# Two-layer state-space vision block: column stores collected over a whole image, images held in pairs of chunks, first tap by channel tile, one table load for 1 / std in the last image

## The chip, the cores and the metric

The kernel runs on one core of a Trainium2 chip. The metric is the device time of one execution in microseconds; the time of a kernel is the median of its runs. The profile comes from one further execution, whose own time is given beside its span.

## What is computed

The input x has 8 images of 64 x 64 positions and 192 channels. Two layers follow each other; each adds to x the output of one block applied to the group-normalized x (32 groups). Cut to what matters, with D = 384 inner channels and L = 4096 positions of an image:

```python
xz = einsum('bhwc,ec->bhwe', gn(x), in_proj_w); xx, z = split(xz)
xc = silu(depthwise_conv3x3(xx) + conv_b)
xs = directions(xc)           # rows, rows reversed; layer 1 also columns, columns reversed
dts, Bs, Cs = split(x_proj_weight @ xs)
delta = softplus(dt_w @ dts + dt_b)
h = exp(delta * A) * h + (delta * u) * B      # step by step along the L positions, 16 states
y = sum(h * C) + xs * Ds                      # summed over the directions
y = layernorm(y) * ln_w + ln_b
x = x + out_proj_w @ (y * gate(z))            # gate: gelu in layer 0, silu in layer 1
```

Layer 0 scans in two directions (along rows, both ways), layer 1 in four (rows and columns, both ways). So layer 1 needs xc in two orders: by rows (`xcd`) and by columns (`xcd_col`).

## The kernel before

The work of each layer is a front and then scans, one layer after the other. The four parts run on the same core; a layer's scans begin when its front has ended.

**Tiling.** An image is cut into 8 chunks of T = 512 positions (8 rows of 64). The 384 inner channels are three channel tiles (dt) of 128 partitions. The 192 input channels lie in `x1` (the first 128 on 128 partitions, 16 KB each) and `x2` (the other 64, with even chunks on the lower and odd chunks on the upper 64 partitions). Both are held for a whole image, twice (`bufs=2`). `load(b)` (L232) reads an image with four DMAs for x1 and two for x2, all on SP's queue.

**The front** (`front`, L206) is under a manual schedule: each engine runs its instructions in the order in which `order()` (L414) emits them. The loop there takes one pair of chunks, 2p and 2p+1, per pass (32 passes for 8 images). A pass holds, in this order:

- `conv(b, 2p)` (L357): the later taps of the depthwise convolution as block-diagonal matmuls into `pc`, then the sum of the first taps (`tp`) added through the mask matrix; Silu on ACT into `xo`; the store of `xo` to `xcd` on SP's queue. In layer 1, ACT then copies each channel tile of the chunk, turned to columns, into `xw` (L377). An `xw` tile covers four chunks (`HC = 4`); with the fourth, ACT issues its store to `xcd_col` (L384), in runs of 32 floats.
- for each channel tile: `project` (L315) of the next pair, which is four matmul groups into two of the four `pi` buffers and two copies into `pad` (on DVE, and on ACT for the third tile in layer 0); `turn` (L386) of the chunk before, which transposes a tile of `xo` on PE into a `pi` buffer and copies it to `xv` on ACT.
- in layer 0 `x_proj` (L400) of the chunk before.
- `first` (L342) of the next pair's first chunk: the first tap on ACT, for all three channel tiles; `second` (L349): the other early taps on DVE, three per channel tile in layer 1 and four in layer 0. They read `pad` and build `tp`.
- `conv(b, 2p+1)`, `turn` of chunk 2p, in layer 0 `x_proj` of chunk 2p, and `first` and `second` of the next pair's second chunk; the third channel tile's `second` of that chunk is left for the next pass.

Between these stand the steps for the next image's group statistics: `stats` (L251, DVE, 12 per image), `means`, `group_means` and `variances` (L267 to L295, with small matmuls that spread the group values and a Sqrt on ACT, which needs a table load), and `normalize` (L297, ACT, in place on x1 and x2). `load(b + 2)` is issued in pass p=2.

**The scans** (`scans`, L503) go through steps of one chunk in one direction. A dictionary of slots sets the place of each function within a step; `L0_SLOTS`, `L0_LAST`, `L1_SLOTS` and `L1_LAST` hold the slot numbers. Per slot, a decay Exp on ACT (L712), a scan on DVE (L736), a product on POOL (L737) and matmuls on PE run together. Ready output chunks go through the `f_` functions. In the last image (`last`), whose chunks are finished one per step, `f_rstd` (L884) computes 1 / std as Exp(-0.5 Ln(v)), and `f_act` (L893) applies the gate to z. In layer 0, `f_act` is in slot 18 and `f_rstd` in slot 19. In layer 1 they are in slots 22 and 17. `dt_softplus` (L629) ends with a preload of the table set that holds ln and exp.

Of the kernel before, what the change touches and what calls it, by code (L numbers as in the profile page):

```python
# [8 lines left out]
F32 = mybir.dt.float32  # L9
# [6 lines left out]
P = 128  # L16
B = 8
H = 64
W = 64
L = H * W  # L20
# [4 lines left out]
DT = 3  # L25
NS = 16
T = 512
# [6 lines left out]
NP = NS // 2  # L34
NG = NS // 2
S = (G + 1) * NG
HC = 4
GN_EPS = 1e-5
LN_EPS = 1e-5

# [165 lines left out]
def front(tc, name, x_src, xcd, xcd_col, xtd, xdd, w_in, t, clear, consts):  # L206
# [9 lines left out]
    with tc.tile_pool(name=f"{name}_a1", bufs=1) as a1, tc.tile_pool(  # L216
# [12 lines left out]
                nc.vector.tensor_scalar_mul(taps[:, dt, s - NV, :], mask, cw[:, dt, s : s + 1])  # L229
        ims = {}  # L230

        def load(b):  # L232

            im = ims[b] = {
                "x1": a2.tile([P, L], F32, name="x1"),
                "x2": a2.tile([P, NH, T], F32, name="x2"),
                "bst": a2.tile([P, NCH + NH, 6], F32, name="bst"),
            }
            for q in range(4):
                sl = slice(q * (L // 4), (q + 1) * (L // 4))  # L240
                nc.sync.dma_start(out=im["x1"][:, sl], in_=x_src[b][:P, sl])
            for r in range(2):
                nc.sync.dma_start(
                    out=im["x2"][r * G : (r + 1) * G],
                    in_=x_src[b][P:].rearrange("p (c r t) -> r p c t", r=2, t=T)[r],
                )

        def part_of(im, n):
            return im["x1"][:, n * T : (n + 1) * T] if n < NCH else im["x2"][:, n - NCH]

        def stats(b, *ns):  # L251
            for n in ns:
                nc.vector.bn_stats(ims[b]["bst"][:, n], part_of(ims[b], n))
# [61 lines left out]
        def project(b, p, dt):  # L315

            im = ims[b]
            pi = [psa.tile([P, T], F32, name="pi", bufs=4) for r in range(2)]
            cols = slice(dt * P, (dt + 1) * P)
            for r in range(2):  # L320
                nc.tensor.matmul(  # L321
                    pi[r], w_x1[:, cols], part_of(im, 2 * p + r), start=True, stop=False
                )
            for r in range(2):
                rows = slice(r * G, (r + 1) * G)
                nc.tensor.matmul(
                    pi[r],
                    w_x2[rows, cols],
                    im["x2"][rows, p],
                    start=False,  # L330
                    stop=True,
                    tile_position=(r * G, 0),
                )
            for r in range(2):
                c = 2 * p + r
                copy = nc.scalar.copy if dt == 2 and xdd is not None else nc.vector.tensor_copy
                copy(
                    pad[:, dt, 1 + c * RB : 1 + (c + 1) * RB, 1 : W + 1],
                    pi[r].rearrange("p (h w) -> p h w", w=W),
                )  # L340

        def first(b, c):  # L342

            tp = ims[b]["tp", c] = a2.tile([P, DT, T], F32, name="tp")
            for dt in range(DT):
                tv = tp[:, dt].rearrange("p (h w) -> p h w", w=W)
                nc.scalar.activation(tv, window(dt, c, 0), AF.Identity, scale=cw[:, dt, 0:1])  # L347

        def second(b, c, *dts):  # L349
            for dt in dts:  # L350
                tv = ims[b]["tp", c][:, dt].rearrange("p (h w) -> p h w", w=W)
                for s in range(1, NV):
                    nc.vector.scalar_tensor_tensor(  # L353
                        tv, window(dt, c, s), cw[:, dt, s : s + 1], tv, ALU.mult, ALU.add
                    )

        def conv(b, c):  # L357
            pc = psa.tile([P, DT, T], F32, name="pc")
            for s in range(NV, 9):
                for dt in range(DT):  # L360
                    block_diag(
                        nc, pc, taps[:, dt, s - NV, :], window(dt, c, s), dt, s == NV, False
                    )
            for dt in range(DT):
                block_diag(nc, pc, mask, ims[b]["tp", c][:, dt], dt, False, True)
            xo = ims[b]["xo", c] = a2.tile([P, DT, T], F32, name="xo")
            for dt in range(DT):
                nc.scalar.activation(xo[:, dt], pc[:, dt], AF.Silu, bias=cb[:, dt : dt + 1])  # L368
            nc.sync.dma_start(out=xcd[b].rearrange("(t p) l -> p t l", p=P)[:, :, c * T : (c + 1) * T], in_=xo)
            if xcd_col is None:  # L370
                return
            part, at = divmod(c, HC)
            if at == 0:
                ims[b]["xw"] = [a2.tile([P, W, HC * RB], F32, name="xw", bufs=5) for dt in range(DT)]
            for dt in range(DT):
                xw = ims[b]["xw"][dt]
                nc.scalar.copy(  # L377
                    xw[:, :, at * RB : (at + 1) * RB],
                    xo[:, dt].rearrange("p (h w) -> p w h", w=W),
                )  # L380
                if at == HC - 1:
                    xwv = xcd_col[b].rearrange("(t p) (w h) -> p t w h", p=P, h=H)
                    rows = slice(part * HC * RB, (part + 1) * HC * RB)
                    nc.scalar.dma_start(out=xwv[:, dt, :, rows], in_=xw)  # L384

        def turn(b, c, dt):  # L386
            im = ims[b]
# [25 lines left out]

        def order():  # L414

            stats(0, *range(NCH + NH))
            means(0)
            group_means(0)
            deviations(0)
            variances(0)  # L420
            normalize(0, 0)
            for dt in range(DT):
                project(0, 0, dt)
            for c in range(2):
                first(0, c)
                second(0, c, *range(DT))
            normalize(0, 1, 2, 3)
            if B > 1:
                load(1)
            early_stats = ((4, 5), (8, 9)), ((), (4, 5, 6, 7))  # L430
            late_stats = ((6, 7), (10, 11)), ((0, 1, 2, 3), (8, 9, 10, 11))
            prev = None
            for g in range(B * NH):
                b, p = divmod(g, NH)
                more = b + 1 < B
                n, q = divmod(g + 1, NH)
                go = g + 1 < B * NH
                conv(b, 2 * p)
                for dt in range(DT):
                    if go:  # L440
                        project(n, q, dt)
                    if dt == 0 and prev:
                        second(b, 2 * p + 1, 2)
                    if prev:
                        turn(*prev, dt)
                    if p == 2 and more and dt == 1:
                        group_means(b + 1)
                if p == 2 and more:
                    deviations(b + 1)
                if prev and xdd is not None:  # L450
                    x_proj(*prev)
                if go:
                    first(n, 2 * q)
                    second(n, 2 * q, *range(DT))
                if p < 2 and more:
                    stats(b + 1, *early_stats[b == 0][p])
                conv(b, 2 * p + 1)
                for dt in range(DT):
                    turn(b, 2 * p, dt)
                if xdd is not None:  # L460
                    x_proj(b, 2 * p)
                if p == 2 and more:
                    variances(b + 1)
                    normalize(b + 1, 0)
                if go:
                    first(n, 2 * q + 1)
                    second(n, 2 * q + 1, 0, 1)
                if p < 2 and more:
                    stats(b + 1, *late_stats[b == 0][p])
                if p == 1 and more:  # L470
                    means(b + 1)
                if p == 3 and more:
                    normalize(b + 1, 1, 2)
                if p == 0 and b:
                    normalize(b, 3)
                if p == 2 and b + 2 < B:
                    load(b + 2)
                if p == 3 and b + 2 < B:
                    stats(b + 2, *range(4))
                prev = b, 2 * p + 1  # L480
            for dt in range(DT):
                turn(*prev, dt)
            if xdd is not None:
                x_proj(*prev)

        load(0)
        if clear:
            zero = a1.tile([P, T * S // G // 8], F32, name="zero")
            nc.gpsimd.memset(zero, 0.0)
# [13 lines left out]
def scans(tc, name, x_src, x_dst, xcd, xcd_col, xtd, xdd, t, dirs, rank, row_b, gate, slots, last, consts, dram):  # L503
# [33 lines left out]
    with tc.tile_pool(name=f"{name}_s1", bufs=1) as s1, tc.tile_pool(  # L537
# [352 lines left out]
                fin["y"], fin["y"], fin["pv"].unsqueeze(1).to_broadcast([P, DT, T])  # L890
            )

        def f_act():  # L893
            nc.scalar.activation(fin["g"], fin["g"], gate)

        def f_affine(dt):
            nc.scalar.activation(  # L897
# [92 lines left out]
        for c in range(NCH):  # L990
# [20 lines left out]
            for w, (src, key) in enumerate((("y", "pm"), ("sq", "pv"))):  # L1011
                thrice(e, own["f_mean"][w], f_mean, src, key)
            for f in f_center, f_square, f_rstd, f_scale, f_act:
                at(e, own[f.__name__], f, *((c == NCH - 1,) if f is f_square else ()))
            for dt in range(DT):
                at(e, own["f_affine"][dt], f_affine, dt)
                at(e, own["f_times"][dt], f_times, dt)
# [144 lines left out]
```

## Time and profile before

| | us |
|---|---|
| runs, median of 3 | 26029.92 (26021.06 to 26032.92) |
| profiled execution, own time | 26028.44 |
| its span, first to last instruction | 26026.6 |
| front of layer 0 | some 20 to 985 |
| front of layer 1 | some 9192 to 10317 |
| an image in the front of layer 0 (between equal places in successive images) | 119.6 |
| an image in the front of layer 1 (mean of seven) | 138.1 |

Over the whole span PE is busy for 24190.1 us (93%), DVE 24270.1 (93%), POOL 22104.7 (85%) and ACT 17787.7 (68%). These shares are those of the scans, which fill most of the span. The front has to be read in stretches of its own. A line of a timeline gives the start, the time from the first start to the last end of the merged instructions, the engine, the line of the kernel, and in brackets the idle time before it with what ended it. PEq, ACTq and SPq are the engines' instruction queues: time spent on issuing a DMA is there. A line of a chain gives the start, the length and what ran; the chain is the work that ended last, followed back.

### The profile page before, as it was taken

To read this page: it belongs to the slowest core of one execution; us is meant where nothing else is said; L and a number is where in the kernel's file an instruction comes from. 1 tells how busy PE (TensorE), PEld (TensorE's weight loads), DVE (VectorE), ACT (ScalarE), POOL (GpSimd) and SP (SyncE) were. 2 spreads that over 40 slices of the span, in tenths; PEclk is the share of its full clock that TensorE was granted. 3 is DMA by queue.
4 is the path that set the end of the run, shared out by engine and by line. 5 is a ranking of instruction groups with operands and counts; after the bars stand their busy time and mean duration, and the time that the engine had idled before them with its cause. 6 is when DMAs were issued, how large, how long until landed. Compare 5 with 4: busy or idle time off the path is not lost.

```text
span 26026.6 us, 785972 instructions
## 1 busy us (share of the span) xinstructions
PE 24190.1 (93%) x340032; PEld 13575.8 (52%) x340032; DVE 24270.1 (93%) x22142; ACT 17787.7 (68%) x28084; POOL 22104.7 (85%) x9615
## 2 busy tenths in 40 slices
PE   8999999999999877999999999999999999999999
PEld 4455555555555533555555555555555555555554
DVE  7899999999999855999999999999999999999998
ACT  4567777777777655666767767767767767767766
POOL 0399999999999701999999999999999999999997
PEclk9999999999999988999999999999999999999999
DMA  4566666666666556576576576576576576576574
GB/s 153 145 154 158 153 154 154 155 158 155 156 155 154 136 149 159 163 161 166 164 164 166 164 163 166 163 163 166 163 164 167 163 163 167 164 163 167 164 163 140
DMA packets 4225339, 4140.59 MB, mean 159 GB/s; under 512 B 2532524, under 2 KB 2732868, under 8 KB 4221892
## 3 DMA queue, kind: packets, MB, share of 16 engines
q1 hardware_dynamic: 3819760, 4032.72, 60.1%
q10 hardware_dynamic: 402132, 57.59, 1.3%
q8 instruction: 2692, 44.11, 0.7%
q14 instruction: 755, 6.18, 0.1%
HBM read 3443.63 MB, written 645.99 MB: 157 GB/s over the span
## 4 chain that ended last, share of the span: by engine, by line
PE 40%; DVE 38%; ACT 10%; issue 9%; ACTq 1%; DMA 1%; POOL 0%; SPq 0%; DVEq 0%; POOLq 0%
DVE h L736 33%; PE hb L695 17%; PE py L152 11%; ACT da L712 3%; PE pt L608 2%; PE pz L835 2%; PE pd L560 2%; PE po L912 2%; DVE tp L353 2%; DVE dut L658 1%; ACT delta L145 1%; ACT L145 1%; PE pc L152 1%; ACT L632 1%; ACTq L384 1%
## 5 line engine op out<-in xcount | busy, mean ns | idle before, releaser
L737 POOL TENSOR_TENSOR hc<-h,cr 128x1024 f32<-128x1024 f32 x9216 | 21639.8, 2370 | 3773.7 <-DMA xt_k<-xtd 2178.2
L736 DVE TENSOR_TENSOR_SCAN h<-da,st,hb 128x512 f32<-128x512 f32 x16128 | 19187.5, 1258 | 629.8 <-PE hb L695 560.6
L712 ACT ACTIVATE da<-delta,a_neg 128x512 f32<-128x512 f32 x18432 | 12142.9, 713 | 3225.2 <-DVE h L736 3218.7
L695 PEld LDWEIGHTS hb<-dg,dut 64*128 64x128 f32 x147456 | 9260.3, 186 | 7083.1 <-issue 5877.6
L695 PE MATMUL hb<-dg,dut 64*128 64x128 f32 x147456 | 10909.6, 287 | 908.9 <-DVE h L736 639.5
L152 PE MATMUL py<-hc,mask 32*32 32x512 f32 x147456 | 6882.8, 603 | 0.2
L152 PEld LDWEIGHTS py<-hc,mask 32*32 32x32 f32 x147456 | 1571.9, 103 | 2348.3 <-issue 1770.6
L736 DVE TENSOR_TENSOR_SCAN h<-da,hb 128x512 f32<-128x512 f32 x2304 | 2611.8, 1199 | 135.1 <-PE hb L695 122.4
L742 ACT COPY st<-h 128x6 f32<-128x6 f32 x2688 | 532.9, 198 | 1844.2 <-DVE h L736 1843.7
L353 DVE SCALAR_TENSOR_TENSOR tp<-pad,cw,tp 128x512 f32<-128x512 f32 x1344 | 991.0, 750 | 592.3 <-ACT tp L347 537.8
L608 PE MATMUL pt<-xdbl,w_dt 96*128 96x512 f32 (+1 forms) x2304 | 1302.9, 647 | 49.5 <-DVE yc L878 34.9
L650 PE MATMUL pq<-ident,delta 128*128 128x128 f32 x4608 | 760.4, 288 | 387.7 <-DVE dut L658 333.7
L622 ACT ACTIVATE delta<-pt,dtb 128x512 f32<-128x512 f32 x1152 | 783.9, 681 | 485.4 <-PE pt L608 485.3
L835 PE MATMUL pz<-xn_sq,w_in 96*128 96x512 f32 x1536 | 826.1, 637 | 38.0 <-ACT xn_sq L823 14.8
L658 DVE TENSOR_TENSOR dut<-pq,xt_k 128x512 f32<-128x512 f32 x1152 | 765.8, 665 | 88.2 <-PE pq L650 88.2
L560 PE MATMUL pd<-x_k,w_x 128*128 128x512 f32 x1536 | 798.3, 629 | 30.9 <-DVE yc L878 15.1
L912 PE MATMUL po<-yc,w_out 128*96 128x512 f32 x1536 | 787.4, 624 | 16.8 <-POOL yc L906 15.0
L650 PEld LDWEIGHTS pq<-ident,delta 128*128 128x128 f32 x4608 | 485.2, 141 | 586.9 <-DVE dut L658 472.7
L321 PE MATMUL pi<-x,w_x 128*128 128x512 f32 x768 | 427.0, 664 | 313.7 <-ACT x L301 124.1
L906 POOL TENSOR_TENSOR yc<-yc,g 128x512 f32<-128x512 f32 x384 | 491.0, 1281 | 126.4 <-ACT yc L897 123.6
L152 PE MATMUL pc<-pad,taps 32*32 32x512 f32 x13824 | 575.9, 592 | 12.2 <-ACT xo L368 12.2
L145 ACT ACTIVATE delta<-delta 128x1536 f32<-128x1536 f32 x384 | 570.5, 1486 | 4.3
(105 smaller groups left out, 9921.3 us busy)
## 6 DMA issues: line engine op xcount, KB each, us to landing
cr<-cscr SPq DMA_DIRECT2D x2048, 512.0 KB
dg<-dgd SPq DMA_DIRECT2D x1536, 512.0 KB
cr<-xdd SPq DMA_DIRECT2D x1024, 512.0 KB
xt_k<-xtd SPq DMA_DIRECT2D x768, 384.0 KB
xcd<-xo SPq DMA_DIRECT2D x128, 768.0 KB
xtd<-xv SPq DMA_DIRECT2D x128, 768.0 KB
y<-yrow SPq DMA_DIRECT2D x128, 768.0 KB
yc<-yrow SPq DMA_DIRECT2D x128, 768.0 KB
```

Source lines behind the costliest of these rows:

```text
L145: nc.scalar.activation(out, in_, AF.Softplus)
L152: nc.tensor.matmul(out[j * Q : (j + 1) * Q, dt], w[i * Q : (i + 1) * Q], x[i * Q : (i + 1) * Q], start=first, stop=last, tile_position=(i ...
L353: nc.vector.scalar_tensor_tensor(tv, window(dt, c, s), cw[:, dt, s : s + 1], tv, ALU.mult, ALU.add)
L560: nc.tensor.matmul(live[i]["pd"][:R], w_x[:, dt, k, :], live[i]["x"][:, dt], start=(dt == 0), stop=(dt == DT - 1),)
L608: nc.tensor.matmul(pt, w_dt[:, k, dt * P : (dt + 1) * P], live[i]["xdbl"][:rank], start=True, stop=True,)
L650: nc.tensor.transpose(pq[:, g], live[i]["delta"][:, dt, g * P : (g + 1) * P], ident)
L695: nc.tensor.matmul(hv[:, r, q], live[i]["dut"][r * G : (r + 1) * G, dt, q], dg[r * G : (r + 1) * G, q, :, 2 * mm : 2 * mm + 2], start=True ...
L712: nc.scalar.activation(da[:, n].rearrange("p (r g j) -> p r g j", r=2, j=G), live[i]["delta"][:, dt].rearrange("p (g r j) -> p r g j", r=2 ...
L736: nc.vector.tensor_tensor_scan(o, a, v, init, ALU.mult, ALU.add)
L737: nc.gpsimd.tensor_mul(hc[:, dt], h[:, dt], live[i]["cr", m])
L835: nc.tensor.matmul(fin["pz"], w_in[:, u, dt * P : (dt + 1) * P], fin["xn"][:, u], start=(u == 0), stop=(u == CT - 1),)
L912: nc.tensor.matmul(fin["po"][:CP], w_out[:, dt, u * CP : (u + 1) * CP], fin["y"][:, dt], start=(dt == 0), stop=(dt == DT - 1),)
```

## The change

1. `load` takes pairs of chunks. `x1` and `x2` become tiles of one pair (4 KB and 2 KB a partition) with six buffers each. A pair is read with one DMA for x1 and two for x2. Pairs 0 and 1 of the next image but one are read at the end of pass p=3, pairs 2 and 3 of the next image in pass p=0. The order of the statistics follows, and none is left in p=3.
2. The copies to columns leave `conv` and become `columns(b, p)`, which takes both chunks of the pair after `conv(b, 2p+1)`, the turns and `x_proj`. An `xw` tile covers the whole image, with one buffer per channel tile, and its store is issued in p=3.
3. `first` takes channel tiles and is called behind each tile's `project` and `turn`. `second` of chunk 2p+1 is left for the next pass for the last two channel tiles, behind the projections.
4. In the last image, `f_act` ends with a preload of the table set with ln and exp.

```diff
-        def load(b):
+        def load(b, *ps):
+            im = ims.setdefault(b, {})
+            for p in ps:
+                if p == 0:
+                    im["bst"] = a2.tile([P, NCH + NH, 6], F32, name="bst")
+                im["x1", p] = a2.tile([P, 2 * T], F32, name="x1", bufs=6)
+                im["x2", p] = a2.tile([P, T], F32, name="x2", bufs=6)
+                sl = slice(2 * p * T, 2 * (p + 1) * T)
+                nc.sync.dma_start(out=im["x1", p], in_=x_src[b][:P, sl])
+                for r in range(2):
+                    nc.sync.dma_start(
+                        out=im["x2", p][r * G : (r + 1) * G],
+                        in_=x_src[b][P:, (2 * p + r) * T : (2 * p + r + 1) * T],
+                    )
...
-        def first(b, c):
+        def first(b, c, *dts):
+            if 0 in dts:
+                ims[b]["tp", c] = a2.tile([P, DT, T], F32, name="tp")
+            for dt in dts:
+                tv = ims[b]["tp", c][:, dt].rearrange("p (h w) -> p h w", w=W)
                 nc.scalar.activation(tv, window(dt, c, 0), AF.Identity, scale=cw[:, dt, 0:1])
...
+        def columns(b, p):
             if xcd_col is None:
                 return
-            part, at = divmod(c, HC)
-            if at == 0:
-                ims[b]["xw"] = [a2.tile([P, W, HC * RB], F32, name="xw", bufs=5) for dt in range(DT)]
+            if p == 0:
+                ims[b]["xw"] = [a2.tile([P, W, H], F32, name="xw", bufs=DT) for dt in range(DT)]
             for dt in range(DT):
                 xw = ims[b]["xw"][dt]
-                if at == HC - 1:
-                    nc.scalar.dma_start(out=xwv[:, dt, :, rows], in_=xw)
+                for c in 2 * p, 2 * p + 1:
+                    nc.scalar.copy(
+                        xw[:, :, c * RB : (c + 1) * RB],
+                        ims[b]["xo", c][:, dt].rearrange("p (h w) -> p w h", w=W),
+                    )
+                if p == NH - 1:
+                    nc.scalar.dma_start(
+                        out=xcd_col[b].rearrange("(t p) (w h) -> p t w h", p=P, h=H)[:, dt], in_=xw
+                    )
...
         def order():
-            stats(0, *range(NCH + NH))
+            stats(0, *(n for p in range(NH) for n in (2 * p, 2 * p + 1, NCH + p)))
...
             for dt in range(DT):
                 project(0, 0, dt)
-            for c in range(2):
-                first(0, c)
-                second(0, c, *range(DT))
+                first(0, 0, dt)
+                second(0, 0, dt)
+            first(0, 1, *range(DT))
+            second(0, 1, 0)
             normalize(0, 1, 2, 3)
             if B > 1:
-                load(1)
+                load(1, 0, 1)
+            sets = {
+                (0, 0): (0, 1), (0, 1): (8, 2), (1, 0): (3, 9, 4), (1, 1): (5, 10, 6, 7, 11)
+            }
...
                 for dt in range(DT):
                     if go:
                         project(n, q, dt)
-                    if dt == 0 and prev:
-                        second(b, 2 * p + 1, 2)
                     if prev:
                         turn(*prev, dt)
+                    if go:
+                        first(n, 2 * q, dt)
...
+                if p == 0 and more:
+                    load(b + 1, 2, 3)
+                second(b, 2 * p + 1, 1, 2)
...
                 if go:
-                    first(n, 2 * q)
                     second(n, 2 * q, *range(DT))
+                if more and (p, 0) in sets:
+                    stats(b + 1, *sets[p, 0])
                 conv(b, 2 * p + 1)
                 for dt in range(DT):
                     turn(b, 2 * p, dt)
                 if xdd is not None:
                     x_proj(b, 2 * p)
+                columns(b, p)
                 if p == 2 and more:
                     variances(b + 1)
                     normalize(b + 1, 0)
                 if go:
-                    first(n, 2 * q + 1)
-                    second(n, 2 * q + 1, 0, 1)
+                    first(n, 2 * q + 1, *range(DT))
+                    second(n, 2 * q + 1, 0)
+                if more and (p, 1) in sets:
+                    stats(b + 1, *sets[p, 1])
...
-                if p == 2 and b + 2 < B:
-                    load(b + 2)
                 if p == 3 and b + 2 < B:
-                    stats(b + 2, *range(4))
+                    load(b + 2, 0, 1)
...
-        def f_act():
+        def f_act(rstd_next=False):
             nc.scalar.activation(fin["g"], fin["g"], gate)
+            if rstd_next:
+                nc.scalar.preload_act_table_set("natural_log_exp_and_others")
...
+                flag = {f_square: (c == NCH - 1,), f_act: (True,)}
+                at(e, own[f.__name__], f, *flag.get(f, ()))
```

## Prediction

> **What bounds the kernel now.** I read the page's slices first: two fronts, 20 to 985 us (layer 0) and 9192 to 10317 us (layer 1), with POOL at 0; between and behind them lie the scans, of which the change touches only the last images' table loads. Busy time in stretches of one image then shows that no engine is full in the layer 1 front, while PE nearly is in layer 0.
>
> ```profile
> 378.00:498.00 120.00, 112.13 (x1244) 52.85 (x1250) 88.59 (x133) 62.22 (x103) 0.00 (x0) 1.00 0.44 151
> 9495.50:9633.00 137.50, 102.13 (x1376) 50.78 (x1376) 75.88 (x118) 77.07 (x112) 0.00 (x0) 0.90 0.63 161
> ```
> (Columns: stretch, length, busy PE, PEld, DVE, ACT, POOL, PE clock, DMA share, GB/s.) What leaves layer 1's engines empty is in the chain of waits, over one half image:
>
> ```profile
> 9403.67 0.52 ACTq L384
> 9404.23 1.11 ACT xw L377
> 9405.37 7.46 ACTq L384
> 9412.87 1.07 ACT xw L377
> 9413.96 6.02 ACTq L384
> ```
> ACT stands still while it issues the column stores (L384): 0.56 + 7.5 + 6.1, about 14.2 us, twice per image. These pieces are the chain itself, so nothing covers them. Downstream, PE stands idle for want of the normalized x that ACT still owes:
>
> ```profile
> 9632.26 2.22 ACT L301 ACTIVATE x<-x,gnb,grs 128x512 f32<-128x512 f32 x3
> 9633.13 1.22 PE L321 MATMUL pi<-x,w_x 128*128 128x512 f32 x1 [15.66 <-ACT x L301]
> ```
> In layer 0 the chain is mostly DVE tp L353, and PE waits twice per pair of chunks for the pad copies, which stand behind the taps in DVE's order:
>
> ```profile
> 428.16 1.27 DVE L337 COPY pad<-pi 128x512 f32<-128x512 f32 x2
> 428.89 1.12 PE L321 MATMUL pi<-x,w_x 128*128 128x512 f32 x2 [1.40 <-DVE pad L337]
> 433.11 1.13 PE L321 MATMUL pi<-x,w_x 128*128 128x512 f32 x2 [0.59 <-DVE pad L337]
> ```
> In the last image of layer 0, three table loads stand ahead of the 1/std, and the chain runs through them:
>
> ```profile
> 8636.78 1.28 ACT L712 ACT_TABLE_LOAD   x1
> 8639.43 1.28 ACT L885 ACT_TABLE_LOAD   x1
> 8641.40 1.28 ACT L886 ACT_TABLE_LOAD   x1
> 8643.31 1.75 DVE L889 TENSOR_TENSOR yc<-yc,pm 128x1536 f32<-128x1536 f32 x1 [3.15 <-ACT pm L886]
> ```
>
> **What the Trainium skill says.** "DMA: Bandwidth & Descriptors", Specifications, asks for at least 512 B per piece for full rate. The trace agrees: over the layer 1 front the column queue moves 393984 packets of 128 B, and the other queue long ones:
>
> ```profile
> q1 hardware_dynamic: 68338, 122.31, 32.0%
> q10 hardware_dynamic: 393984, 50.33, 29.3%
> ```
> (packets, MB, share of 16 engines in 1110 us): 122.31/(0.320 x 1110) = 344 GB/s against 50.33/(0.293 x 1110) = 155 GB/s. "ScalarE: Activation LUTs", Table sets, says that natural_log_exp_and_others holds ln and exp, so one load serves both; its section on ACT_TABLE_LOAD gives 1283 ns, and the trace shows 1283 ns at each. The drain of 1380 ns that it adds is not seen: the Ln follows its load at 8640.72.
>
> **The change, part by part.** A pair is one pass of order(): conv(2p), three projections of the next pair q with the turns of the chunk before, conv(2p+1), the turns of 2p. Layer 1 durations from the traced groups: conv 5.72; projection 1.72 + 1.06 and turn 0.59, 3.37 per channel tile; three in a row of Silu 1.84, of xv 1.5, of first tap 1.94, of normalize 2.22; a column copy 1.02; a tap 0.757, a pad copy 0.61, a stats 0.64.
>
> *Column stores.* 48 issues become 24 of 2.1 MB, with runs of 16 KB instead of 128 B. No row shows such an issue. SP's issues of 2 to 4 KB runs take 0.35 to 0.8; I take 0.55, the low end 0.35. The high end is that the second and third still wait for the one before to drain: 2.1 MB / 344 GB/s = 6.1 us each, 12.2 per image. So 28.4 us of issue go and 1.65 come.
>
> *Column copies collected.* Their number stays 6 per pair, but all six now stand behind conv(2p+1) and the turns, ahead of first(2q+1) and of normalize on ACT. This gives part of the gain back. A copy writes the same runs of 8 floats, now 256 B apart instead of 128; no row shows that. Bounds: a plain copy's 0.59 and, as far above, 1.45; I take 1.02, since shape and runs stay. I lay out a pair from C, the end of conv(2p+1). PE: turns to 1.5, conv(2q) when Silu has freed pc, 2.0 to 7.75, three projections 10.1, conv 5.85: 23.85 with its joints. ACT: Silu to 1.95, xv to 3.45, six copies to 9.6, first tap from there. DVE: taps of 2q to 6.2, early stats, one tile of 2q+1 from 10.3 to 12.6, late stats, then the pad copy. The second projection needs that copy's first half at 11.95, since pi has four buffers.
> - p=0: two late stats, copy at 14.55: +2.6, 26.45.
> - p=1: five late stats and the aggregates, copy at 17.0: +5.05, and the group means 1.7: 30.6.
> - p=2: spread 1.2, then table load, Sqrt, three small DVE steps and normalize give x at 12.55 where PE wants it at 8.95: +3.6; pad copy +0.75: 29.4.
> - p=3: with the issues the first normalized chunk is there at 13.9, wanted at 7.75: +6.15, 30.0.
>
> Sum 116.5 per image. Before, seven images run from 9228.85 to 10195.48, 138.1 each: 21.6 x 7 = 151. In the last image one stall goes (14.2) and the later taps cost 2.6: 11.6. The end, where the scans' start waited for the column DMA (10281 to 10317), has 6.3 MB to move instead of 3.1, at twice the rate: -4, between -10 and +8. The start, with taps between projections: -1. **Layer 1: 168.**
>
> *First tap by channel tile, taps moved behind the projections.* In layer 0 each pair loses its two PE waits. The second half projection came 1.57 and 0.75 late against PE's own pace, 29.13 - 2.32 = 26.8. DVE then has its 20 taps (15.2 us) after the pad copies, done 22.8 us after the loop's start, where conv(2q) wants them at 25.6, so they are covered; ACT has its first tap ready, being 52% busy. Four pairs 107.2, spreads 3.4, and p=1 with its five late stats +1.5: 112.1 against 119.63 from 139.09 to 856.91 (six images): 45. The other eight pairs give 13 and the start 4, where taps no longer wait for all three projections. **Layer 0: 62**, down to 0 if PE finds another wait.
>
> *Loads in pairs.* 12 issues per image on SP instead of 6, some 5 us; SP waits between its stores for ACT (477.6 us in six images), so they are hidden, and nobody queues behind them but stores with 20 us to spare. Six buffers suffice: a slot's last reader, the projection, is past when the load is issued. The load ahead of p=0 lands beside 6.3 MB of columns: 7.9 MB at 344 GB/s is 23 us, and stats want it at some 36. Nothing, at most 3 us per image.
>
> *Three xw buffers.* Copies of the next image wait for the last store. Issued by 11.25, wanted from 33: 6.3 MB plus some 3 MB of stores need 27. Covered, by little.
>
> *Table load.* In seven chunks of layer 0 three loads become one. The 1/std moves up by 2.57, but its sum is ready only at some 8640.0, so 2.0 of it counts: 14. Layer 1 has softplus's preload ahead of its 1/std, except in its second last chunk (wait 5.2 instead of 3.2): 2. In each layer's last chunk the load at L886 stood open: 2 x 1.3. **19.** The added preload takes the place of L712's load; at layer 1's end it makes one more Silu load, beside the mean. Cover gone, the cost is 1.3.
>
> **Sum:** 168 + 62 + 19 = 249. The profiled execution took 26028.44 (span 26026.6 and 1.8 around): 25779. The runs' median is 1.5 above it: 25781.
>
> **Rivals.**
> 1. *The regrouping costs nothing*, only stalls leave: 138.1 - 28.4 = 109.7, 47 us more than the forecast: 25734. For it: before, p=0 ran in 25.3. Against: six copies in a block are 6.1 us ahead of normalize.
> 2. *The large issue blocks too*: 12.2 x 7 = 85 less: 25866. For it: a single SP issue of 4 KB runs took 1.73 us, so bytes can hold an issue. Against: most take 0.5.
> 3. *Layer 0 gives nothing* because a DVE or ACT wait takes the place of the pad wait: 25843. For it: the chain there is DVE. Against: DVE is 74% busy.
> 4. *Slower*: xw has one set for a whole image, so the copies at p=0 wait if the stores drain slowly. They are wanted at C + 37 at the last tile; to lose all three gains, layer 1's image must reach 138.1 + 93/7 = 151, a stall of 35 us, so stores that end at C + 72: 6.3 MB in 66 us, under 95 GB/s. At 80 GB/s, 79 us, the stall is some 47, the image 164: 26.9 x 7 - 93 = +95, 26125. Against: even 128 B packets drained at 155.
> 5. *It doesn't do what it says*: the preload is followed by L712's load as well. 11 us back: 25792.
>
> **How the numbers follow.** Forecast with rival 5 0.64; rival 1 0.12; rival 2 0.12; rival 3 0.06; a mix that leaves nothing measurable 0.02; rival 4 0.04. Some 0.2% (52 us) is what a measurement here can tell from no change. Faster by more: 0.94; within: 0.02; slower: 0.04. The range goes from rival 1 to rival 2: 25730 to 25870.
>
> **What would show it.** L384 with 24 issues under 1 us each; DMA share of the layer 1 front below 0.5 at a higher GB/s; images near 116 us in layer 1 and 112 in layer 0; PE pi waits on ACT x of some 6 us once per image and on DVE pad of some 5 in p=2; no ACT_TABLE_LOAD at L885 and L886. Issues of 6 us, ACT xw waiting for a DMA, or layer 1 images above 125 would make it wrong.

## The result, and the profile after

The changed kernel takes **25,835.58 us** (median of 6 runs, 25,810.22 to 25,844.72); the kernel before, measured beside it, 26,024.96 (26,009.67 to 26,032.92). The ratio is 0.9927, 95% interval [0.9914, 0.9939]. That is 189 us less, inside the range of the prediction and 55 us above its forecast. The profiled execution has a span of 25,835.2 us, 191.4 less than before. Four marks in the two traces cut it into stages: the first state matmul (hb) of layer 0, the first projection of layer 1, the first hb of layer 1, the end.

| stage, us | before | after | difference | predicted |
|---|---|---|---|---|
| start to the first hb of layer 0 | 1023.3 | 952.6 | -70.7 | -62 |
| to the first projection of layer 1 | 8175.2 | 8141.3 | -33.9 | about -15 |
| front of layer 1, to its first hb | 1136.8 | 1051.9 | -85.0 | -168 |
| to the end | 15691.3 | 15689.5 | -1.8 | about -3 |

Of the 33.9 in the second stage, 20.9 lie in the last image, behind its first gate (564.6 us before, 543.7 after). The other 13 can't be put down to the change: in runs 7 and 6 below this stage is 8145.3 and 8191.3 us, in two kernels that leave its code alone. So the front of layer 0 and its table loads gave some 14 us more than forecast (70.7 and 20.9 against 62 and 15), and the front of layer 1 gave half.

One image of each layer after the change, in the table of stretches (length; busy PE, PEld, DVE, ACT, POOL; PE clock, DMA share, GB/s):

```profile
246.29:356.99 110.70, 110.18 (x1234) 53.27 (x1234) 88.97 (x133) 62.41 (x104) 0.00 (x0) 1.00 0.46 163
9482.80:9612.60 129.80, 104.94 (x1388) 51.58 (x1376) 76.15 (x118) 77.56 (x111) 0.00 (x0) 0.92 0.46 171
```
Layer 0: PE is busy in 110.18 of 110.70 us, so both pad waits are gone and none has come in their place. Layer 1: 129.8 in this stretch, 129.4 as the mean of six images from first column store to first column store, where 116.5 was forecast; PE is still idle for 25 us, at a mean clock of 0.92.

The column queue, on the page, and the column stores of image 0 on ACT, in the timeline (start, duration, instruction, in brackets the idle time before it and what ended it):

```profile
q10 hardware_dynamic: 11604, 57.59, 0.6%
```
```profile
9225.31 0.34 ACTq L386 DMA_DIRECT2D xcd_col<-xw  x1
9225.69 2.09 ACT L381 COPY xw<-xo 128x512 f32<-128x512 f32 x2 [0.41 <-ACT xw L381]
9227.81 0.33 ACTq L386 DMA_DIRECT2D xcd_col<-xw  x1
9228.18 2.01 ACT L381 COPY xw<-xo 128x512 f32<-128x512 f32 x2 [0.41 <-ACT xw L381]
9236.33 0.33 ACTq L386 DMA_DIRECT2D xcd_col<-xw  x1
9236.70 1.95 ACT L349 ACTIVATE tp<-pad,cw 128x512 f32<-128x512 f32 x3 [6.51 <-DMA xcd_col<-xw]
```
A store of 2.1 MB is issued in 0.33 us (0.55 was taken). But the third is issued only at 9236.33, although its copies end at 9230.19: ACT stands still for 6 us first (the 6.51 of the last line counts the 0.33 of the issue too), and "<-DMA xcd_col<-xw" says that a column store ended that. In the waits of ACT over the front of layer 1 the same line sums to

```profile
ACT tp L349 <- DMA xcd_col<-xw: 41.6, 6, 8.1
```
(us in total, times, longest): six times, in images 0 to 5. Image 6 has no such wait:

```profile
10006.72 0.33 ACTq L386 DMA_DIRECT2D xcd_col<-xw  x1
10007.09 1.95 ACT L349 ACTIVATE tp<-pad,cw 128x512 f32<-128x512 f32 x3 [0.40 <-ACT xw L381]
```
What that wait does to PE, behind the stores of image 0:

```profile
9239.41 3.78 PE L322 MATMUL pi<-x,w_x 128*128 128x512 f32 x4 [11.81 <-ACT x L302]
...
9245.03 1.88 PE L322 MATMUL pi<-x,w_x 128*128 128x512 f32 x4
```
PE waits 11.81 us for the normalized x, and the first four matmuls then take 3.78 us, twice the 1.88 that the same four take a little later. In the stretches, 9239 to 9243 has a PE clock of 0.50:

```profile
9239.00:9243.00 4.00, 3.59 (x4) 1.17 (x4) 0.75 (x1) 4.00 (x7) 0.00 (x0) 0.50 0.98 413
```

And the gate with the new preload in the last image of layer 0 (timeline of ACT):

```profile
8629.07 1.28 ACT L902 ACT_TABLE_LOAD   x1
8630.37 1.49 ACT L902 ACTIVATE g<-g 128x1536 f32<-128x1536 f32 x1
8631.86 1.28 ACT L904 ACT_TABLE_LOAD   x1
...
8635.13 0.66 ACT L893 ACTIVATE pm<-pm,eps_ln 128x512 f32<-128x512 f32 x1 [0.54 <-PE pm L860]
8635.83 0.58 ACT L894 ACTIVATE pm<-pm 128x512 f32<-128x512 f32 x1
```
The Ln and the Exp follow each other with no load between; what the Ln waits for is PE's sum (0.54), so the preload is fully covered.

**Theory** for the missing 83 us of layer 1: (T1) the third column store waits for the first one to land, because it takes the completion counter that the first one took; (T2) the waits that are left let TensorE's clock fall, and the projections behind them run at half speed. **Rivals**: the queue itself holds a third large store until data has drained; the collected copies cost more than forecast; the slow matmuls merely wait for inputs.

For T1 the program's own list of semaphore waits speaks. It has eight completion counters for the DMAs (DMAHW0 to DMAHW7), handed out in rotation in the order in which the scheduler expects the DMAs. In image 0:

```
xcd_col0<-xw, first store    waits Activation            counts on DMAHW2, to 7008
xcd_col0<-xw, second store   waits DMAHW0, Activation    counts on DMAHW0
xcd_col0<-xw, third store    waits DMAHW2 >= 7008, Activation
```
The six loads of image 2 have counters 3, 4, 5, 6, 7 and 1: five lie between the first and the second store and one between the second and the third, so the first store stands eight places ahead of the third, and the value that the third waits for is the one the first brings. In images 6 and 7 nothing is left to load: the third store waits for no counter in image 6, and in image 7 for that of an older store to another tensor. A page of the Trainium skill, "DMA: Bandwidth & Descriptors", section "Anatomy of one DMA — SWDGE (gpsimd) path", says that DMA engines don't wait for semaphores, and that any such wait is made on the issuing sequencer, before dispatch. The trace agrees for a store issued by ACT: the wait stands on ACT's own timeline, with the first tap and the normalisation queued behind it.

### The profile page after: what moved, and what is told of

Same layout as the page of the kernel before. It is cut to its first block, busy times and chain, and to the rows that moved or that the text cites. A ratio compares the mean times of both kernels' runs of the same rounds, so it can differ in the third digit from the quotient of the medians.

```text
span 25835.2 us, 786127 instructions
## 1 busy us (share of the span) xinstructions
PE 24166.5 (94%) x340032; PEld 13568.7 (53%) x340032; DVE 24275.9 (94%) x22142; ACT 17771.4 (69%) x28068; POOL 22094.0 (86%) x9615
## 4 chain that ended last, share of the span: by engine, by line
DVE 25%; PE 24%; issue 6%; ACT 6%; DMA 0%; POOL 0%; DVEq 0%; SPq 0%; ACTq 0%; POOLq 0%
DVE h L744 23%; PE hb L703 11%; PE py L151 7%; PE pd L568 2%; PE pt L616 2%; ACT da L720 2%; DVE dut L666 1%; PE pz L843 1%; ACT delta L144 1%; PE po L922 1%; ACT L144 1%; ACT L640 1%; ACT delta L630 1%; PE pq L658 0%; ACT xn_sq L831 0%
## 5 line engine op out<-in xcount | busy, mean ns | idle before, releaser
L922 PE MATMUL po<-yc,w_out 128*96 128x512 f32 x1536 | 782.8, 620 | 15.4 <-POOL yc L916 12.4
L322 PE MATMUL pi<-x,w_x 128*128 128x512 f32 x768 | 407.2, 650 | 165.9 <-ACT x L302 116.5
```

The lines of the kernel that those rows point to most:

```text
L922: nc.tensor.matmul(fin["po"][:CP], w_out[:, dt, u * CP : (u + 1) * CP], fin["y"][:, dt], start=(dt == 0), stop=(dt == DT - 1),)
```

## The experiments

Runs are compared by median and by the stages of their profiles. The kernel before was run beside each: 26,014 to 26,016 us.

**1. The load one pair earlier** (T1 against the queue). From the changed kernel:

```diff
-                if p == 3 and b + 2 < B:
+                if p == 2 and b + 2 < B:
                     load(b + 2, 0, 1)
```


> The load of the first two pairs of image b + 2 stands at the end of pair 2 in place of pair 3, so that its six DMAs no longer lie between the first and the third column store of an image. Theory (the third store waits for the first one to land because it takes the completion counter that the first one took, eight DMAs earlier): the wait of 6 to 8 us of the first tap for the column stores is gone in all images of layer 1, the stretch from pair 3 to pair 0 falls from 39.3 to about 33 us in six images, and the matmuls that ran at half clock after it run in 1.9 us in place of 3.8; the image of layer 1 falls from 129.6 to 120 to 123 us, in sum 40 to 60 us less than the changed kernel, about 25,785 us. Rival (the queue takes the third store only when the data of the first has drained, whatever the counters): the wait stays, 25,836 within 10 us.

Measured: **25,797.95 us**, ratio to before 0.9917 [0.9902, 0.9932]; 38 us under the changed kernel. The front of layer 1 falls from 1051.9 to 1011.5, an image (from first store to first store, mean of six) from 129.4 to 122.9. The same store in the timeline of ACT:

```profile
9474.03 0.33 ACTq L386 DMA_DIRECT2D xcd_col<-xw  x1
...
9476.52 0.33 ACTq L386 DMA_DIRECT2D xcd_col<-xw  x1
...
9478.92 0.33 ACTq L386 DMA_DIRECT2D xcd_col<-xw  x1
9479.30 1.95 ACT L349 ACTIVATE tp<-pad,cw 128x512 f32<-128x512 f32 x3 [0.40 <-ACT xw L381]
```
The third store is issued 4.9 us after the first, where it was 11.0, with no wait. So the queue takes three stores of 2.1 MB one behind the other, and T1 stands: the wait came from where six loads stood in the program. The gain, 38 us, is just under the 40 to 60 expected, and one part of the expectation failed: the matmuls did not come back to 1.9 us. After a wait of half the length the four still take twice their time (timeline of PE):

```profile
9482.00 3.78 PE L322 MATMUL pi<-x,w_x 128*128 128x512 f32 x4 [5.70 <-ACT x L302]
```

**2. The copies back beside the convolutions** (what collecting them costs). In the changed kernel, columns() goes back into conv(), one chunk at a time:

```diff
             nc.sync.dma_start(out=xcd[b]..., in_=xo)
+            if c == 0:
+                ims[b]["xw"] = [a2.tile([P, W, H], F32, name="xw", bufs=DT) for dt in range(DT)]
+            for dt in range(DT):
+                nc.scalar.copy(ims[b]["xw"][dt][:, :, c * RB : (c + 1) * RB], ...)
+                if c == NCH - 1:
+                    nc.scalar.dma_start(out=xcd_col[b]..., in_=ims[b]["xw"][dt])
...
-                columns(b, p)
```


> The changed kernel with the column copies back beside the convolution of each chunk (three at a time, right behind the Silu), the whole-image buffers and their three stores kept. Theory (collecting six copies ahead of the first taps and the normalisation is what holds the image of layer 1, through ACT and then through TensorE's clock): the four pairs of a layer 1 image come near the 23.85 us of a pair without a store, the image takes 96 to 104 us in place of 129.6, and the time is 190 to 240 us under the changed kernel, about 25,620 us. Rival (only the wait of the third store and its aftermath matter; where the copies stand is worth what the prediction gave it, 3.6 to 6 us a pair at most, and TensorE's clock stays low): 116 us an image, 25,740 us. Second rival (copies right behind the Silu delay the turns and so the xo buffers): no gain.

Measured: **25,762.81 us**, 0.9904 [0.9889, 0.9918]. An image takes 119.4 us: not the theory's 96 to 104, but near the first rival's 116. The third store no longer waits for a counter here (the scheduler lays it elsewhere), but another wait has come, in the first chunk of the next image:

```profile
9458.70 1.07 ACT L378 COPY xw<-xo 128x512 f32<-128x512 f32 x1
9460.55 1.06 ACT L378 COPY xw<-xo 128x512 f32<-128x512 f32 x1 [0.78 <-DMA xcd_col<-xw]
9465.91 1.05 ACT L378 COPY xw<-xo 128x512 f32<-128x512 f32 x1 [4.31 <-DMA xcd_col<-xw]
```
The copies overwrite buffers whose stores, issued at 9445.99 to 9449.06, are still under way; the last has landed by 9465.9, so 6.3 MB took 19.9 us, 316 GB/s beside the other traffic. That is the mechanism of the prediction's rival 4, here with 35 us of waiting on ACT over the front instead of a loss. Run 3 tests whether taking the copies late in pair 0 is what keeps it away.

**3. Late in pair 0, early in the others.** Chunks 2 to 7 are copied beside their convolution, chunks 0 and 1 where the change put them:

```diff
+            if c > 1:
+                columns(b, c)
...
-                columns(b, p)
+                if p == 0:
+                    columns(b, 0, 1)
```


> The changed kernel with the column copies of chunks 2 to 7 back beside their convolution, those of chunks 0 and 1 kept where the change put them, late in pair 0. Theory (late copies in pair 0 give the stores of the image before the time to land; late copies in pairs 1 to 3 only hold up ACT): no wait of a copy for a store, no wait of the third store, and the image of layer 1 at 111 to 116 us, 25,700 to 25,740 us. Rival (six copies in one piece in pair 0 hold up the first taps by as much as the wait for the stores did, 5 us and the clock behind it): 118 to 121 us an image, 25,750 to 25,775 us.

Measured: **25,733.56 us**, 0.9892 [0.9878, 0.9907]; an image takes 116.6 us (mean of six), and no copy and no store waits for a store. The time lies within the theory's range, the image just above it, and the rival's 118 to 121 is not reached. Against run 1, which collects all copies and has no wait for a column store either, the front of layer 1 is 48.8 us shorter (962.7 against 1011.5), 6.3 us an image between first stores: so much do the collected copies of pairs 1 to 3 cost, with the stores behind them, where the prediction's delays in these pairs sum to 15.6. The rest is not given back: PE still waits elsewhere, 2.0 us for pad copies in one pair and 2.0 for xv in another.

**4. PE kept busy in the waits** (T2 against inputs). To run 1 are added matmuls that nobody reads, in a free part of the bank of pg:

```diff
                 conv(b, 2 * p)
+                if xcd_col is not None and ((p == 0 and b) or (p == 3 and more)):
+                    for k in range(14 if p == 0 else 9):
+                        nc.tensor.matmul(
+                            ims[b if p == 0 else b + 1]["warm"], w_x1[:, :P], w_x1, start=True, stop=True
+                        )
```


> The kernel with the load one pair earlier, and besides matmuls on w_x1 whose result nobody reads, in the two waits for the normalised image in layer 1: 14 of 128x128 by 384 columns ahead of the projection of pair 1 (a wait of 5.7 us), 9 ahead of that of pair 0 of the next image (a wait of 3.7 us). Theory (TensorE's clock falls in those waits, and the projections after it pay): the first four projection matmuls take 1.9 to 2.0 us in place of 3.5 to 3.8, the image of layer 1 falls from 122.6 to 118 to 119.5 us, 20 to 32 us less in sum than with the load alone, about 25,770 us. Rival (the slow matmuls wait for their inputs, and the clock is only how that is shown): the four still take over 3.4 us, and the time is the same or up to 20 us more.

Measured: **25,843.98 us**, 0.9937 [0.9923, 0.9952], 46 us *slower* than run 1. The unread matmuls were too many, and the projection behind them still points to T2 (timeline of PE):

```profile
9505.48 9.30 PE L450 MATMUL pg<-w_x 128*128 128x384 f32 x28
9514.61 1.88 PE L324 MATMUL pi<-x,w_x 128*128 128x512 f32 x4
```
Each such matmul appears as two records and takes 0.66 us, not 0.35, so 14 fill 9.3 us of a wait of 5.7. But the projection behind them takes 1.88: at full clock. Its inputs had been ready for some 3.6 us by then, so the second try has to settle whether they mattered. It has 8 and 2 unread matmuls in place of 14 and 9, so that the projection again starts as soon as its input is there.

> As the run with unread matmuls in the two waits, but sized to them: there one matmul took 0.66 us, twice what it was counted at, so that they outlasted the waits by 3.6 and 4.6 us. Now 8 ahead of the projection of pair 1 (5.3 us of 5.7), 2 ahead of that of pair 0 of the next image (1.3 us, behind a wait of 2.2 for the Sqrt that reads the same bank). Theory (the clock that falls in these waits costs 1.6 to 2.4 us behind each): the first projection matmuls at 1.9 us, the image of layer 1 at 118 to 120 us in place of 122.6, 18 to 32 us less in sum than with the load alone, about 25,772 us. Rival (the work behind waits for VectorE and ACT anyway, so that a faster projection only waits longer): 122 us an image, 25,798 us within 8.

Measured: **25,769.34 us**, 0.9906 [0.9890, 0.9923], 29 us under run 1. Most images take 119.8 to 120.0 us, two 122.2. Only part of the 29 can be pinned to this stage: over seven images, from store to store, it is 16 us, over the whole front 12.4. The first projection:

```profile
9462.72 5.43 PE L450 MATMUL pg<-w_x 128*128 128x384 f32 x16
9468.52 1.98 PE L324 MATMUL pi<-x,w_x 128*128 128x512 f32 x4 [0.38 <-ACT x L304]
```
Here the projection starts behind a wait of 0.38 us for the normalized x, as in run 1 with its inputs just there, and takes 1.98 where it took 3.78. So T2 stands and the rival falls, but only the first of the two places gains: the two matmuls ahead of the next image's pair 0 come behind a wait of 2.2 us, and the projection there still takes 3.04 us.

**5. The same in run 3.** Four unread matmuls ahead of the projection of pair 1 and three ahead of the second channel tile of pair 2 (the p, dt of the loop are 0, 0 and 1, 1):

```diff
                 for dt in range(DT):
+                    if xcd_col is not None and b and (p, dt) in ((0, 0), (1, 1)):
+                        for k in range(4 if p == 0 else 3):
+                            nc.tensor.matmul(ims[b]["warm"], w_x1[:, :P], w_x1, start=True, stop=True)
```


> The kernel with the copies of chunks 0 and 1 late and those of 2 to 7 beside their convolution, and besides unread matmuls in two waits of layer 1: 4 ahead of the projection of pair 1 (2.65 us in a wait of 2.85), 3 ahead of the second channel tile of the projection of pair 2 (2.0 us in a wait of 2.0). Theory (the clock, as above): the matmuls behind the two waits at 1.9 us in place of 3.5 and 3.8, the image of layer 1 from 116 to 111 to 113 us, 20 to 35 us less than without them, about 25,705 us. Rival (the path of these pairs runs over ACT and VectorE, not over the projections): 25,733 us within 8.

Measured: **25,717.23 us**, 0.9887 [0.9872, 0.9902]. The fastest of all, 118 us under the changed kernel, but its interval overlaps that of run 3, and the medians differ by 16 us where 20 to 35 were expected. In the profile four of six images take 112.7 to 113.2 us, the front of layer 1 is 15.6 us shorter than in run 3. Not all comes through: in one image of 116.8 us PE falls to half clock at another wait, 2.03 us for xv. At the same place in run 3, behind the same shorter waits of 0.6 and 0.5 us, it does not (first line run 5, second run 3):

```profile
9547.62 3.65 PE L324 MATMUL pi<-x,w_x 128*128 128x512 f32 x4 [2.03 <-ACT xv L401]
```
```profile
9546.00 1.98 PE L322 MATMUL pi<-x,w_x 128*128 128x512 f32 x4 [2.02 <-ACT xv L399]
```

**6. The first taps alone**, in the kernel before:

```diff
                     if go:
                         project(n, q, dt)
-                    if dt == 0 and prev:
-                        second(b, 2 * p + 1, 2)
                     if prev:
                         turn(*prev, dt)
+                    if go:
+                        first(n, 2 * q, dt)
...
+                second(b, 2 * p + 1, 1, 2)
...
-                    second(n, 2 * q + 1, 0, 1)
+                    second(n, 2 * q + 1, 0)
```


> The kernel before with the first tap by channel tile and the second taps moved, nothing else of the change. Theory (the layer 0 gain is this part's alone): the image of layer 0 falls from 119.64 to 110.7 us as in the changed kernel, 8.9 x 7 = 63 us less than before there, and layer 1's front within 10 us either way; about 25,960 us. Rival (the loads in pairs also free layer 0's pair 1): 112 to 116 us an image, 25 to 50 us less.

Measured: **25,937.18 us**, 0.9969 [0.9956, 0.9981]. In the profile, taken of the longest of its six executions (25,962.92), the first hb of layer 0 is at 943.7 us, 79.6 earlier than before, and the front of layer 1 takes 1134.0 against 1136.8. The image of layer 0 falls to 110.0:

```profile
241.40:351.40 110.00, 110.00 (x1235) 53.45 (x1234) 89.13 (x133) 62.38 (x105) 0.00 (x0) 1.00 0.47 164
```
PE has no idle time left. The theory holds: the gain in layer 0 is this part's, and up to the first hb the changed kernel keeps 9 us less of it.

**7. The loads in pairs alone**, in the kernel before: load(), part_of(), the order of the statistics.

```diff
-                if p == 2 and b + 2 < B:
-                    load(b + 2)
-                if p == 3 and b + 2 < B:
-                    stats(b + 2, *range(4))
+                if p == 3 and b + 2 < B:
+                    load(b + 2, 0, 1)
...
+                if p == 0 and more:
+                    load(b + 1, 2, 3)
...
+                if more and (p, 1) in sets:
+                    stats(b + 1, *sets[p, 1])
```


> The kernel before with its images loaded in pairs of chunks, with the statistics' order that belongs to it, nothing else of the change. Theory (the pairs gain nothing and cost a little in layer 0: the changed kernel's first scan starts 8.9 us later than with the taps alone): first scan of layer 0 at 1030 to 1036 us in place of 1023.3, front of layer 1 1130 to 1140 us as before, in sum 5 to 12 us more than before. Rival (the pairs are part of layer 0's gain): first scan at or under 1015 us.

Measured: **26,051.9 us**, 1.0014 [1.0007, 1.0021]: slower than before by 37 us, three times what was expected. First hb at 1069.1 us, 45.8 later, where 7 to 13 were expected; the front of layer 1 as before (1133.6). Some 6 us of it lie at the start and 6.6 in each of six images. The place in these lies between pairs 1 and 2, in the timelines of DVE and of PE:

```profile
370.74 6.12 DVE L355 SCALAR_TENSOR_TENSOR tp<-pad,cw,tp 128x512 f32<-128x512 f32 x8
376.78 3.06 DVE L255 BATCH_NORM_STATS2 bst<-x 128x6 f32<-128x512 f32 x5
...
380.14 1.22 DVE L339 COPY pad<-pi 128x512 f32<-128x512 f32 x2
```
```profile
380.83 2.08 PE L323 MATMUL pi<-x,w_x 128*128 128x512 f32 x2 [4.12 <-DVE pad L339]
```
Eight taps and five statistics stand ahead of the pad copies; PE waits 4.12 us (1.74 before the change), and then falls to half clock:

```profile
381.00:392.00 11.00, 11.00 (x30) 6.17 (x30) 5.21 (x11) 0.59 (x1) 0.00 (x0) 0.50 0.01 1
```
In the changed kernel four taps stand there instead of eight, the pad copy comes in time, and the pairs cost 8.9 us up to the first hb (952.6 against 943.7), 4 of them at the start. Neither part's effect is what it is alone; they do not add.

**8. The preload alone**, in the kernel before:

```diff
-        def f_act():
+        def f_act(rstd_next=False):
             nc.scalar.activation(fin["g"], fin["g"], gate)
+            if rstd_next:
+                nc.scalar.preload_act_table_set("natural_log_exp_and_others")
```


> The kernel before with the table load for Ln and Exp put behind the gate's Silu in the last image, nothing else. Theory: two loads of 1.28 us fewer on the path in each of the eight chunks of layer 0's last image (564.6 us to 545 us there), 19 to 21 us less than before, about 26,004 us. Rival (the loads hide beside VectorE): 0 to 6 us less.

Measured: **25,995.1 us**, 0.9991 [0.9983, 1.0000]: 21 us less, with an interval that reaches to no change. The stretch where it acts, from the gate in the last image of layer 0 to the first projection of layer 1, is 541.4 us against 564.6 before, 564.2 with the taps alone and 560.5 with the pairs alone. So the trace shows some 20 us, which the run's time alone can't.

## Why the prediction was right, and where it was not

**The sum came within its range in part by luck.** The two fronts missed in opposite directions, and the upper end of the range was set by rival 2, a block at every large issue, which did not come; another wait, at one store in three, cost part of what rival 2 had allowed for.

**Column stores: right.** 24 issues of 0.33 us where 0.55 was taken; 27 us of issue per image are gone. Rival 2's wait was thought of as a queue that must drain before the next issue; run 1 shows that it need not for stores of this form.

**Layer 1 images: wrong, 129.4 where 116.5 was forecast**, and above the 125 that the prediction named as its own refutation. By the starts of the column copies the four pairs of image 1 took 26.7, 32.2, 31.0 and 39.3 us where the sum had 26.45, 30.6, 29.4 and 30.0. Pair 0 is right; the figures for pairs 1 and 2 are 1.6 us too low each. The failed step is the one for p=3, "with the issues the first normalized chunk is there at 13.9": it counted every instruction of ACT's queue, but not that an issue can have a wait of its own. *Loads in pairs* failed with it, in "they are hidden, and nobody queues behind them": nobody queues behind the loads on SP, but their places in the rotation of the counters make a store on ACT wait for another. Run 1 gives that 6.5 us per image in six images, 40 us of the front in all. The rest of the step was right: without the wait for the store PE waits 5.70 us for the normalized x (run 1), where the sum had 6.15.

The other missing term is the clock. All steps for PE used full-clock durations, while the prediction itself left PE waits of 3.6 to 6 us in the image. "TensorE: Matmul & The Clock Gate", section "What's actually happening", gives the window after which an idle TensorE runs at half rate as about 3.4 us. The trace agrees: 5.7 and 11.8 us of waiting are both followed by matmuls at 3.78 in place of 1.88. It also shows half speed after a shorter wait, 2.03 us in run 5, and full speed after one of 2.02 at the same place in run 3, so neither the length of the last wait nor the gaps before it decide alone; what else does stays open. The table of stretches of the kernel before had the sign in it, a clock of 0.90 in layer 1 against 1.00 in layer 0. Run 4 gives this term 12 to 16 us of the front. Together 52 to 56 of 83 us. With both terms gone, in the second try of run 4, the four pairs take 27.5, 32.6, 30.8 and 30.2 us (means of six): the failed step is back at its 30.0. The other 27 to 31 us, some 4 an image, lie in pairs 0 to 2, and which part of them is clock that the unread matmuls did not reach and which is delay on ACT stays open.

**Column copies collected: right in direction, its split wrong.** The delays of pairs 1 to 3 were to cost 15.6 us; undoing them gives 6.3 (run 3), since the base of 23.85 us a pair, laid out without any other wait, is not reached: 116.6 an image is left where three times the base and pair 0 sum to 98. Rival 1, that regrouping costs nothing, is refuted by the same run.

**Three xw buffers: "Covered, by little" held**, though its own figures don't show it: 11.25 and 27 make 38, past the 33, unless the 27 are counted from the first issue. No copy waited for a store. The margin was larger than thought: in run 2 three stores had landed 19.9 us after the first was issued, and in run 1 the next image's copies start 30.6 us after it. With the copies of pair 0 up to one pair earlier, as in run 2, the wait is there. In rival 4, which did not come, one product is off: 164 is 25.9 above 138.1, not 26.9, so its figure should be 88 us more than before and not 95.

**First tap: right, somewhat low.** Of 112.1 us for the image 110.7 came; the +1.5 for p=1 did not appear. *Loads in pairs* at "nothing, at most 3 us per image" is right beside the taps (0.8 an image and 4 us at the start), and wrong alone (6.6 an image). It was not tried without pairs: whole-image stores beside two whole images of x need 132.8 KB per partition in the front's pool, where 127.2 are left. That the pairs make room for the stores is argued from these sizes, not shown by a run.

**Table load: right, somewhat low.** Of the 19 forecast 15 were for layer 0, which gave 20.9. In layer 1, where 3 were forecast, the stretch from the first gate of the last image to the end is 488.3 us (488.5 to 491.9 in the other kernels with the preload) against 494.6 before (494.6 and 494.5 in runs 6 and 7, which have none): 3 to 6 us, of which the whole stage shows 1.8. In layer 0 nearly all 2.57 us of a chunk's two loads count, not 2.0 as taken: the Ln waits only 0.54 us for its sum.

## What to carry to other kernels

In this kernel a store was held up by an earlier one that had the same completion counter. When large stores stand close together on a busy engine, look in the program for what each issue waits on, and keep short transfers from being put between them. And when a step is costed with a wait of several microseconds left in PE's path, cost the matmuls behind the wait at half clock too, or fill the wait with unread matmuls, whose own time is measured first.

## What the runs showed of the hardware

- What an issue costs ACT is no fixed price of its pieces. Before, of every three stores of 1 MB in runs of 128 B the first was issued in 0.52 us and the next two in some 7.2 and 6.0, though all three have the same form; after, each of three stores of 2.1 MB in runs of 16 KB took 0.33. An estimate from the prediction's queue line: at 155 GB/s, 1.05 MB drain in 6.8 us, about the length of the long issues, so these may wait for an earlier store to drain. No run tests it.
- In the layer 1 fronts of all eleven profiles, each wait of 5.3 us or more ahead of a projection was followed at once by a matmul at less than full speed. Behind waits of 2.0 to 4.5 us both are found.
- In run 7 a single wait of 4.12 us in a PE that is otherwise busy was followed by 11 us at clock 0.50, in which PE was busy throughout. The wait itself was 2.4 us longer than before; pair and image became 8.7 and 6.6 us longer.
- A float32 matmul of 128x128 by 384 columns took 0.66 us and shows as two records; who counts records as matmuls is out by a factor of two.
